# Gated feed-forward of a graph network on Trainium2: the order of VectorE's sums and splits in three of the four quads, and what GpSimd's last weight split waits for

## The chip, the cores and the metric

One core of a Trainium2 chip runs the whole program. The metric is the device time of one execution in microseconds (us). Its parts are named as in the profile: PE is TensorE's matmuls, PEld its weight loads, DVE is VectorE, ACT is ScalarE, POOL is GpSimd, SP is the engine that issues most DMAs.

## What is computed

The reference takes 1024 nodes with 512 features, normalises them, applies a graph convolution, then four layers of attention and a gated feed-forward network, and a second graph convolution. All is float32. The change lies in the feed-forward part of each layer. There, cut to what matters:

```
for i in range(L):                                   # L = 4, D = 512
    h = h + attention(_ln(h, ln2_w[i], ln2_b[i]), cond, Wq[i], Wk[i], Wv[i], Wo[i])
    u = _ln(h, ln3_w[i], ln3_b[i]) @ geglu_w[i] + geglu_b[i]   # 1024x512 @ 512x4096
    val, gate = jnp.split(u, 2, axis=-1)
    f = val * gelu(gate)                                       # 1024x2048
    h = h + f @ ffo_w[i] + ffo_b[i]
```

## The kernel before

The 2048 columns of `f` are four quarters, r = 0 to 3, of four column blocks of 128 (c = 0 to 3). Products with the gate and value weights are made by a seven-product scheme in the manner of Strassen (products 0 to 6 on sums and differences of blocks), so each block needs sums of products afterwards, and these sums are VectorE's.

**The first quarter** runs in float32, in four objects of class `Quad` (quads 0 to 3 below, c = 0 to 3). Products 0 and 1 are made early. `Quad.rest` makes the other five, each of four 128x512 matmuls (`multiply`, L301), into three PSUM banks b, c and d, and between them VectorE sums:

- product 5 into b, then u2 = b + s1 (the tile `gu`);
- product 6 into c, then u3 = c + u2 (also `gu`);
- product 4 into d, then g1 = d + u3 (`g`), which ScalarE passes through the gelu (L972);
- product 3 is added onto c, so TensorE may begin it only when u3 has read c; then g0 = c + u2;
- product 2 is added onto d, so TensorE may begin it only when g1 has read d; then d = d + u2, and the results fT (L1000, L1001), which go to DRAM.

I write c' and d' for products 3 and 2 (the second ones on banks c and d). All these sums are line L982 of VectorE. They read PSUM. In the trace the five products of a quad are `gb`, `gc`, `gd`, `gc`, `gd` of L301 in this order, so the second `gc` of a quad is c' and the second `gd` is d'.

**The fills.** `fill()` takes the next piece of a list of splits that the later quarters need: each float32 tile of the normalised input is split into a high and a low part. A piece is one VectorE instruction on 128x512 (L1017 writes `gr`, L1025 and L1037 write `gl`; both inputs lie in SBUF), at times with ScalarE work ahead of it (L1012, L1015). Behind each L1037 a GpSimd instruction (L1039) makes a third part. After quads 1, 2 and 3, `sums()` gives GpSimd four instructions on 128x256 (L1081) on the weights of a coming chunk. The order of all VectorE work here is that in which the code issues it. Before the change one fill stands behind u2, u3, g1 and g0 each, and one (in `rest`, the last) behind fT.

**The other quarters** are twelve objects of class `Chunk` (r = 1 to 3), with three matmuls on split operands for each product (L1109). The weights of a chunk are split by ScalarE, VectorE (L1045) and GpSimd (L1050: `gsa`, `gsb`, `gs`). `split_rest` issues the second half of a chunk's weight split, and its GpSimd part is made to wait for the VectorE instruction `split_left.low`. Chunk (3,3) is the last. In its stretch the output stage begins: `output.split(0, ...)` splits the first piece of `f` read back from DRAM by `left_parts`: ScalarE `ah_f` (L318), VectorE `al_f` (L319, 128x1024), GpSimd `as_f` (L321). The output's matmuls are L1252. VectorE's instruction L1127 (`scale_onto`) rewrites a PSUM bank that the chunk's next product is added onto; L1175 and L1177 make fT, L1144 the sums.

Of the kernel before, what the change touches and what calls it, by code (L numbers as in the profile page):

```python
# [15 lines left out]
OP = mybir.AluOpType  # L16
# [5 lines left out]
TINY = 2.0 ** -12  # L22
# [4 lines left out]
def gnn_kernel(  # L27
# [26 lines left out]
    nc = tc.nc  # L54
# [10 lines left out]
    KC = D // P  # L65
# [4 lines left out]
    R = DFF // D  # L70
# [156 lines left out]
    h = [hall[:, nb, :] for nb in range(NB)]  # L227
# [78 lines left out]
    def twelve_bits(t):  # L306
        return t.bitcast(F32R)
# [3 lines left out]

    def left_parts(x, name, t=None):

        parts = [slots_of(len(x), f"{n}_{name}") for n in ("ah", "al", "as")]
        for h, l, s, x in zip(*parts, x):
            nc.scalar.mul(twelve_bits(h), x, INWARD * TINY)  # L318
            nc.vector.scalar_tensor_tensor(twelve_bits(l), h, -1.0 / TINY, x, OP.mult, OP.add)  # L319
            if t:  # L320
                t.tensor_tensor(twelve_bits(s), h, l, OP.subtract)  # L321
                continue
            for k in range(2):
                nc.gpsimd.tensor_tensor(twelve_bits(s)[:, k, :], h[:, k, :], l[:, k, :],  # L324
                                        OP.subtract)
        return parts
# [619 lines left out]
    class Quad:  # L946
# [27 lines left out]
        def rest(self, fill):  # L974
            n, bias = self.n, gcols[:, self.cv:self.cv + 1]
            b, c, d = (bank(f"{x}_{n}") for x in ("gb", "gc", "gd"))
            u2, u3 = (acc_tile(f"g{x}_{n}") for x in ("u2", "u3"))
            g0, g1 = (t512(f"{x}_{n}") for x in ("g0", "g1"))
            f0, f1 = self.f.of(self.c)

            def add(to, x, y):
                self.last = pin(nc.vector.tensor_tensor(to, x, y, OP.add))  # L982

            self.product(5, b, True, pin)
            add(u2, b, self.s1)
            fill()
            self.product(6, c, True, pin)
            add(u3, c, u2)
            fill()
            self.product(4, d, True, pin)  # L990
            add(g1, d, u3)
            self.gate(g1, n)
            fill()
            self.product(3, c, False, pin)
            add(g0, c, u2)
            self.gate(g0, n)
            fill()
            self.product(2, d, False, pin)
            add(d, d, u2)
            pin(nc.vector.scalar_tensor_tensor(f0, self.a, bias, g0, OP.add, OP.mult))  # L1000
            pin(nc.vector.scalar_tensor_tensor(f1, d, bias, g1, OP.add, OP.mult))  # L1001
            self.f.store(self.c)
            fill()
            fill()
# [196 lines left out]
    class Output:  # L1201
# [8 lines left out]
                self.raw[n] = slot(f"fr_{self.l}_{n}")  # L1210
                nc.sync.dma_start(self.raw[n], f_dram[s, 2 * u:2 * u + 2].rearrange("c p n -> p c n"))

        def split(self, n, t=nc.vector):
            if n in self.raw:
                self.f[n] = left_parts([self.raw.pop(n)], f"f_{self.l}_{n}", t)

        def fetch_w(self, u):
            if u < UNITS:
# [206 lines left out]
    for l in range(L):  # L1425
# [231 lines left out]
        f, quads = quads_of(l, 0, left, right)  # L1657
# [28 lines left out]
        def fill(n=1):  # L1686
            for _ in range(n):
                next(parts, None)
# [64 lines left out]
                load()  # L1753
        sum_chunk(2)

        def split_rest(short):
            long = begin_split(0, False)
            next(long, None)
            with waiting_for(split_left.low, mybir.EngineType.Pool):
                for flow in short, long:  # L1760
                    for _ in flow:
                        pass

        output = Output(l)
        ahead = output.ahead()
        before, short = None, iter(())
        for r in range(1, R):
            f = Gated(l, r)
            for c in range(KC):
                n = (r - R + 2) * KC + c  # L1770
                if n == -1:
                    output.fetch_w(0)
                if (r, c) == (R - 1, KC - 2):
                    output.fetch(0)
                chunk = ready.pop(0)
                flow = chunk.steps(lambda: before and sum_chunk(1))
                chunk.f = f
                next(flow)
                if 0 < n < 5:
                    next(ahead)  # L1780
                for _ in islice(short, 2):
                    pass
                next(flow)
                if before:
                    split_rest(short)
                    load()
                for _ in parts:
                    pass
                if (r, c) == (R - 1, KC - 1):
                    with in_order(mybir.EngineType.Activation), in_order(mybir.EngineType.DVE), \  # L1790
                            in_order(mybir.EngineType.Pool):
                        output.split(0, nc.gpsimd)
                    output.fetch(1)
                for step in range(3):
                    if before:
                        next(before, None)
                    next(flow)
                    if step == 1 and not before:
                        split_rest(iter(()))
                        load()  # L1800
                before = flow
                short = begin_split(0, True)
                if n == 0:
                    next(ahead)
# [153 lines left out]
```

## Time and profile before

| | |
|---|---|
| median of 3 runs | 2298.52 us (2296.37 to 2298.68) |
| the profiled execution's own time | 2296.64 us |
| its span in the trace | 2294.9 us |
| granted TensorE clock | 1.000 |
| the four quads of layer 0 | 408 to 447 us in the span |
| the twelve chunks of layer 0 | 446 to 563 us |
| distance of a layer from the next | 529 us |

The profile's page gives busy times over the whole span. The timeline lists instructions in order of time: start, duration, engine, line, operation, tile written and tiles read, shape, count where several are merged; in brackets what the engine waited for before. A VectorE instruction's duration reaches some 0.08 us into the next one's, so spacing of starts is used where instructions follow each other. The four layers repeat: the first stall of the second quad stands at 425.48 in layer 0 and at 1483.01 two layers later.

### The profile page before, as it was taken

The numbers are of one execution on the slowest core, as the hardware profiler recorded it, in microseconds if no ns is written. First come the engines' busy times: TensorE is split into PE (matmuls) and PEld (weight loads), VectorE is DVE, ScalarE is ACT, GpSimd is POOL, SyncE is SP. The second block draws the span as 40 slices with busy tenths as digits, with TensorE's granted clock in tenths as the row PEclk, the third lists the DMA queues.
The fourth block names the chain that finished last, engine by engine and source line by source line (L and its number), as shares of the span: only waits on it lengthen the run. The fifth ranks groups of instructions, "written<-read, shape, count | busy, mean of one in ns | idle before, by whom it ended". The sixth has DMA issues, their size and how long they took to land. (4 is left out here: it accounts for less than half of the span.)

```text
span 2294.9 us, 34482 instructions
## 1 busy us (share of the span) xinstructions
PE 2265.4 (99%) x12496; PEld 1754.5 (76%) x12496; DVE 1734.6 (76%) x3172; ACT 1168.7 (51%) x2245; POOL 747.1 (33%) x647
## 2 busy tenths in 40 slices
PE   8999999999999999999999999999999999999999
PEld 5678887587887888488887888578788888668777
DVE  9886556999986555989987554989987554899965
ACT  7555445565355445465356444556437444556521
POOL 1121213486021224377021222368112112268301
PEclk9999999999999999999999999999999999999999
DMA  6042211234411101133521111133531111043551
GB/s 206 2 152 70 74 61 42 83 120 152 169 46 65 61 29 42 60 119 99 200 92 65 51 38 42 42 107 100 184 138 56 37 52 51 1 129 111 184 173 57
DMA packets 144113, 204.42 MB, mean 89 GB/s; under 512 B 11240, under 2 KB 68912, under 8 KB 143936
## 3 DMA queue, kind: packets, MB, share of 16 engines
q1 hardware_dynamic: 141840, 196.72, 26.0%
q0 software_dynamic: 1376, 4.30, 0.6%
q8 instruction: 103, 1.69, 0.3%
q10 hardware_dynamic: 720, 1.11, 0.1%
q14 instruction: 74, 0.61, 0.1%
HBM read 151.75 MB, written 50.34 MB: 88 GB/s over the span
## 5 line engine op out<-in xcount | busy, mean ns | idle before, releaser
L324 POOL TENSOR_TENSOR as_c<-ah_c,al_c 128x512 fp32r<-128x512 f32 x128 | 197.7, 1574 | 901.0 <-DVE al_c L319 679.9
L1123 ACT ACTIVATE g<-g 128x512 f32<-128x512 f32 x192 | 112.5, 586 | 152.8 <-PE g L1109 151.5
L381 ACT ACTIVATE k<-k 128x512 f32<-128x512 f32 x125 | 73.0, 585 | 193.0 <-PE k L370 193.0
L1252 PE MATMUL fx<-bs_wff,as_f 128*128 128x512 f32 x512 | 159.0, 390 | 0.6 <-DVE as_f L321 0.6
L1252 PE MATMUL fy<-bl_wff,al_f 128*128 128x512 f32 x512 | 158.8, 390 | 0.6 <-DVE al_f L319 0.5
L318 ACT ACTIVATE ah_f<-fr 128x1024 fp32r<-128x1024 f32 x64 | 67.9, 1061 | 177.3 <-PE fy L1252 98.8
L1252 PE MATMUL fy<-bh_wff,ah_f 128*128 128x512 f32 x512 | 157.8, 390 | 0.2 <-ACT ah_f L318 0.2
L386 DVE COPY kT<-k 128x512 f32<-128x512 f32 x54 | 37.2, 689 | 156.8 <-PE k L370 156.8
L370 PE MATMUL v<-bh_wv,ah_c 128*128 128x512 f32 x508 | 140.9, 399 | 0.0
L370 PE MATMUL v<-bs_wv,as_c 128*128 128x512 f32 x508 | 137.1, 393 | 2.6 <-ACT v L381 2.6
L1050 POOL TENSOR_TENSOR gsa<-gha,gla 128x512 fp32r<-128x512 f32 x96 | 124.1, 1315 | 40.2 <-DVE gla L1045 40.2
L370 PE MATMUL v<-bl_wv,al_c 128*128 128x512 f32 x508 | 136.6, 390 | 0.0
L843 ACT ACTIVATE pr<-sc,nmax 128x256 f32<-128x256 f32 x256 | 118.1, 474 | 35.0 <-DVE nmax L838 34.5
L370 PE MATMUL k<-ah_c,bh_wk 128*128 128x512 f32 x500 | 135.1, 392 | 0.0
L381 ACT ACTIVATE v<-v 128x512 f32<-128x512 f32 x127 | 75.0, 591 | 116.9 <-PE v L370 116.9
L370 PE MATMUL k<-as_c,bs_wk 128*128 128x512 f32 x500 | 132.1, 395 | 1.8 <-ACT k L381 1.8
L370 PE MATMUL k<-al_c,bl_wk 128*128 128x512 f32 x500 | 133.8, 389 | 0.0
L1109 PE MATMUL g<-gr,gha 128*128 128x512 f32 x384 | 120.0, 394 | 0.0
L1109 PE MATMUL g<-gr,gsa 128*128 128x512 f32 x384 | 119.9, 393 | 0.0
L1109 PE MATMUL g<-gl,gla 128*128 128x512 f32 x384 | 118.3, 389 | 0.0
L370 PEld LDWEIGHTS v<-bs_wv,as_c 128*128 128x128 f32 x508 | 93.2, 188 | 27.7 <-ACT v L381 5.7
L370 PEld LDWEIGHTS v<-bh_wv,ah_c 128*128 128x128 f32 x508 | 92.6, 188 | 27.9 <-issue 9.2
(321 smaller groups left out, 5814.3 us busy)
## 6 DMA issues: line engine op xcount, KB each, us to landing
f_dram<-fT SPq DMA_DIRECT2D x128, 256.0 KB, 2.1
fr<-f_dram SPq DMA_DIRECT2D x64, 512.0 KB, 4.1
ct<-cond_dram SPq DMA_DIRECT2D x48, 512.0 KB, 4.7
wff<-in_L_gnn_ffo_w_dram SPq DMA_DIRECT2D x32, 512.0 KB, 5.2
gxb<-in_L_gnn_geglu_w_dram SPq DMA_DIRECT2D x96, 128.0 KB, 2.5
gxa<-in_L_gnn_geglu_w_dram SPq DMA_DIRECT2D x96, 128.0 KB, 2.6
cond<-in_L_gnn_cond_dram SPq DMA_DIRECT2D x32, 256.0 KB, 4.2
cond_dram<-ct SPq DMA_DIRECT2D x16, 512.0 KB, 3.3
```

The costliest lines, as they stand in the source:

```text
L318: nc.scalar.mul(twelve_bits(h), x, INWARD * TINY)
L324: nc.gpsimd.tensor_tensor(twelve_bits(s)[:, k, :], h[:, k, :], l[:, k, :], OP.subtract)
L370: pin(nc.tensor.matmul(self.bank, twelve_bits(left[k // 2])[:, k % 2, self.c * P:(self.c + 1) * P], twelve_bits(right[k // 2])[:, k % 2, : ...
L381: nc.scalar.mul(self.bank, self.bank, 1.0 + TINY)
L386: nc.vector.tensor_copy(self.to(), self.bank)
L843: nc.scalar.activation(pr3[:, a, :], ps3[:, a, :], AF.Exp, bias=nmax[:, a:a + 1], accum_out=tot[:, a:a + 1])
L1050: split_left.last = pin(t.tensor_tensor(s_at, h_at, l_at, OP.subtract))
L1109: pin(nc.tensor.matmul(to, self.part(i, which)[:, k, :], self.rights[i][which].bitcast(F32R)[:, k, :], start=start and k == 0, stop=stop a ...
L1123: pin(nc.scalar.mul(to, to, 1.0 + TINY))
L1252: pin(nc.tensor.matmul(to, twelve_bits(left[which][0])[:, k, b * P:(b + 1) * P], twelve_bits(right[which])[:, k, :], start=u == 0 and whic ...
```

## The change

Two things are moved; no computation is added or taken away.

First, `Quad.rest`: in quads 1 and 2 (c = 1, 2) no fill stands between u2 and u3, and two stand behind u3. In quad 0 two fills stand between u2 and u3 where there was one. So all later fills come one place earlier in the list, until in quad 3 the list ends.

Second, at the last chunk `split_rest` is no longer called ahead of `output.split(0, ...)` but from inside it, between `al_f` and `as_f`, and GpSimd's part of it waits for `al_f`.

```
-    def left_parts(x, name, t=None):
+    def left_parts(x, name, t=None, between=None):
...
             nc.scalar.mul(twelve_bits(h), x, INWARD * TINY)
-            nc.vector.scalar_tensor_tensor(twelve_bits(l), h, -1.0 / TINY, x, OP.mult, OP.add)
+            left_parts.low = nc.vector.scalar_tensor_tensor(twelve_bits(l), h, -1.0 / TINY, x,
+                                                            OP.mult, OP.add)
+            if between:
+                between()
...
             self.product(5, b, True, pin)
             add(u2, b, self.s1)
-            fill()
+            at_once = self.c in (1, 2)
+            if not at_once:
+                fill()
+            if not self.c:
+                fill()
             self.product(6, c, True, pin)
             add(u3, c, u2)
+            if at_once:
+                fill()
             fill()
             self.product(4, d, True, pin)
             add(g1, d, u3)
...
-        def split(self, n, t=nc.vector):
+        def split(self, n, t=nc.vector, between=None):
             if n in self.raw:
-                self.f[n] = left_parts([self.raw.pop(n)], f"f_{self.l}_{n}", t)
+                self.f[n] = left_parts([self.raw.pop(n)], f"f_{self.l}_{n}", t, between)
...
-        def split_rest(short):
+        def split_rest(short, behind=None):
             long = begin_split(0, False)
             next(long, None)
-            with waiting_for(split_left.low, mybir.EngineType.Pool):
+            with waiting_for(behind or split_left.low, mybir.EngineType.Pool):
...
+                the_last = (r, c) == (R - 1, KC - 1)
                 if before:
-                    split_rest(short)
+                    if not the_last:
+                        split_rest(short)
                     load()
                 for _ in parts:
                     pass
-                if (r, c) == (R - 1, KC - 1):
+                if the_last:
                     with in_order(mybir.EngineType.Activation), in_order(mybir.EngineType.DVE), \
                             in_order(mybir.EngineType.Pool):
-                        output.split(0, nc.gpsimd)
+                        output.split(0, nc.gpsimd, lambda: split_rest(short, left_parts.low))
                     output.fetch(1)
```

On VectorE, this is quad 1 of layer 0 before the change, from its first fill pair to g1; `gu_0_0_1` is u2 (from bank `gb`) and u3 (from bank `gc`), `g_0_0_1` from `gd` is g1:

```order
L1001 SCALAR_TENSOR_TENSOR fT_0_0_18314<-gd_0_0_18309,gcols,g_0_0_0_18313 128x512
L1037 SCALAR_TENSOR_TENSOR gl_4_18331<-ln3S_0_17701,gr_4_18329 128x512
L1037 SCALAR_TENSOR_TENSOR gl_6_18354<-ln3T_1_0_17699,gr_6_18352 128x512
L982 TENSOR_TENSOR gu_0_0_1_18372<-gb_0_1_18369,gs_0_0_0_18128 128x512
L1037 SCALAR_TENSOR_TENSOR gl_6_18354<-ln3T_1_0_17699,gr_6_18352 128x512
L982 TENSOR_TENSOR gu_0_0_1_18373<-gc_0_1_18370,gu_0_0_1_18372 128x512
L1017 SCALAR_TENSOR_TENSOR gr_5_18383<-ln3S_1_17702,gt_5_0_18385 128x512
L982 TENSOR_TENSOR g_0_0_1_18375<-gd_0_1_18371,gu_0_0_1_18373 128x512
```

The same stretch of VectorE in the changed kernel (lines are numbered 3 or 9 higher there: L985 is L982, L1010 is L1001, L1026 is L1017, L1046 is L1037):

```order
L1010 SCALAR_TENSOR_TENSOR fT_0_0_18314<-gd_0_0_18309,gcols,g_0_0_0_18313 128x512
L1046 SCALAR_TENSOR_TENSOR gl_6_18347<-ln3T_1_0_17699,gr_6_18345 128x512 x2
L985 TENSOR_TENSOR gu_0_0_1_18379<-gb_0_1_18376,gs_0_0_0_18128 128x512
L985 TENSOR_TENSOR gu_0_0_1_18380<-gc_0_1_18377,gu_0_0_1_18379 128x512
L1026 SCALAR_TENSOR_TENSOR gr_5_18365<-ln3S_1_17702,gt_5_0_18367 128x512
L1026 SCALAR_TENSOR_TENSOR gr_5_18365<-ln3S_1_17702,gt_5_1_18391 128x512
L985 TENSOR_TENSOR g_0_0_1_18382<-gd_0_1_18378,gu_0_0_1_18380 128x512
```

u3 has moved ahead of one fill, and the place between u3 and g1 now holds two.

On VectorE in quad 2 of layer 0, before, from fT of quad 1 to g1:

```order
L1025 SCALAR_TENSOR_TENSOR gl_5_18398<-ln3S_1_17702,gr_5_18382 128x512
L1017 SCALAR_TENSOR_TENSOR gr_18412<-ln3S_2_17703,gt_3_0_18414 128x512
L982 TENSOR_TENSOR gu_0_0_2_18433<-gb_0_2_18430,gs_0_0_2_18166 128x512
L1017 SCALAR_TENSOR_TENSOR gr_18412<-ln3S_2_17703,gt_3_1_18417 128x512
L982 TENSOR_TENSOR gu_0_0_2_18434<-gc_0_2_18431,gu_0_0_2_18433 128x512
L1025 SCALAR_TENSOR_TENSOR gl_3_18442<-ln3S_2_17703,gr_18412 128x512
L982 TENSOR_TENSOR g_0_0_2_18436<-gd_0_2_18432,gu_0_0_2_18434 128x512
```

and in the changed kernel (L1034 is L1025):

```order
L1026 SCALAR_TENSOR_TENSOR gr_18405<-ln3S_2_17703,gt_3_0_18407 128x512
L1026 SCALAR_TENSOR_TENSOR gr_18405<-ln3S_2_17703,gt_3_1_18417 128x512
L985 TENSOR_TENSOR gu_0_0_2_18435<-gb_0_2_18432,gs_0_0_2_18166 128x512
L985 TENSOR_TENSOR gu_0_0_2_18436<-gc_0_2_18433,gu_0_0_2_18435 128x512
L1034 SCALAR_TENSOR_TENSOR gl_3_18420<-ln3S_2_17703,gr_18405 128x512 x2
L985 TENSOR_TENSOR g_0_0_2_18438<-gd_0_2_18434,gu_0_0_2_18436 128x512
```

Again u3 follows u2 at once, and two fills stand ahead of g1.

The orders of TensorE and of GpSimd stay as they were. Of the waits on GpSimd, these are the ones at the last chunk of layer 0, before (in brackets the engines whose semaphores are waited for):

```order
L1050 TENSOR_TENSOR gsa_3_3_19545<-gha_3_3_19543,gla_3_3_19544 128x512 [waits DMAHW1_49,DMAHW0_49,Activation_49]
L1050 TENSOR_TENSOR gsa_3_3_19545<-gha_3_3_19543,gla_3_3_19544 128x512
L1050 TENSOR_TENSOR gsb_3_3_19616<-ghb_3_3_19614,glb_3_3_19615 128x512 [waits DVE_49,PE_49]
L1050 TENSOR_TENSOR gs_0_3_3_19613<-gs_0_3_3_19613 128x256 [waits PE_49,Activation_49]
L321 TENSOR_TENSOR as_f_0_0_19637<-ah_f_0_0_19635,al_f_0_0_19636 128x1024 [waits DVE_49]
```

and in the changed kernel (L1059 is L1050, L324 is L321):

```order
L1059 TENSOR_TENSOR gsa_3_3_19545<-gha_3_3_19543,gla_3_3_19544 128x512 [waits DMAHW1_49,DMAHW0_49,Activation_49]
L1059 TENSOR_TENSOR gsa_3_3_19545<-gha_3_3_19543,gla_3_3_19544 128x512
L1059 TENSOR_TENSOR gsb_3_3_19616<-ghb_3_3_19614,glb_3_3_19615 128x512 [waits DVE_49,PE_49]
L1059 TENSOR_TENSOR gs_0_3_3_19613<-gs_0_3_3_19613 128x256 [waits PE_49,Activation_49]
L324 TENSOR_TENSOR as_f_0_0_19635<-ah_f_0_0_19633,al_f_0_0_19634 128x1024 [waits Activation_49]
```

`gsb` still waits for VectorE, but now for `al_f` where it was for the chunk's own low part; `as_f` no longer needs that wait, since it stands behind `gsb`.

Beside this, ScalarE issues one `gt` of the fills ahead of the gate of quad 2, and SP issues the four weight loads of the first chunk in the order gxa, gxa, gxb, gxb (before: gxb, gxa, gxa, gxb).

## Prediction

> **What bounds the kernel now.** I read the page's first part, then what TensorE waits for, then the timeline of TensorE in layer 0.
>
> ```profile
> PE 2265.4 (99%) x12496; PEld 1754.5 (76%) x12496; DVE 1734.6 (76%) x3172; ACT 1168.7 (51%) x2245; POOL 747.1 (33%) x647
> ```
>
> TensorE is busy 2265.4 of 2294.9 us, and the change takes no matmul away. Only TensorE's waits can shrink. The table of waits (us in total, times, longest) has two rows that the change can touch:
>
> ```profile
> PE gc L301 <- DVE gu L982: 4.4, 8, 0.7
> ...
> PE g L1109 <- DVE g L1127: 1.2, 4, 0.3
> ```
>
> Eight waits of c' for u3 are two a layer; four waits of a chunk's matmul for L1127 are one a layer. The timeline of TensorE in quads 1 to 3 shows where the first ones stand:
>
> ```profile
> 416.30 1.88 PE L301 MATMUL gc<-ln3S,wgate 128*128 128x512 f32 x4
> ...
> 423.16 1.88 PE L301 MATMUL gd<-ln3S,ges 128*128 128x512 f32 x4
> 425.48 1.98 PE L301 MATMUL gc<-ln3S,wgate 128*128 128x512 f32 x4 [0.43 <-DVE gu L982]
> 427.30 1.88 PE L301 MATMUL gd<-ln3T,ges 128*128 128x512 f32 x4
> 429.01 1.88 PE L301 MATMUL gb<-ln3S,ges 128*128 128x512 f32 x4
> ...
> 432.45 1.88 PE L301 MATMUL gd<-ln3S,ges 128*128 128x512 f32 x4
> 435.00 1.98 PE L301 MATMUL gc<-ln3S,wgate 128*128 128x512 f32 x4 [0.67 <-DVE gu L982]
> 436.82 1.88 PE L301 MATMUL gd<-ln3T,ges 128*128 128x512 f32 x4
> 438.53 1.88 PE L301 MATMUL gb<-ln3S,ges 128*128 128x512 f32 x4
> ...
> 441.97 1.88 PE L301 MATMUL gd<-ln3S,ges 128*128 128x512 f32 x4
> 443.80 1.56 PE L301 MATMUL gc<-ln3S,wgate 128*128 128x512 f32 x3
> ```
>
> The first row is quad 0's c', before any stall. An undisturbed product begins 1.72 us after the last (438.53 to 441.97 are two steps). c' of quad 1 begins 2.32 later, 0.60 lost, and its successor 1.82 later, 0.10 lost. In quad 2 the same sum is 0.83 + 0.10, in quad 3 0.11 + 0.10. Together 1.84 us a layer, 7.4 us in four: that is all that the first part can bring.
>
> **Part one: u3 earlier, g1 behind two fills.** These are VectorE's and GpSimd's rows in quad 1:
>
> ```profile
> 422.45 0.69 DVE L1037 SCALAR_TENSOR_TENSOR gl<-ln3T,gr 128x512 fp32r<-128x512 f32 x1
> 423.05 0.69 DVE L982 TENSOR_TENSOR gu<-gb,gs 128x512 f32<-128x512 f32 x1
> 423.65 1.17 DVE L1037 SCALAR_TENSOR_TENSOR gl<-ln3T,gr 128x512 fp32r<-128x512 f32 x1
> 424.74 0.68 DVE L982 TENSOR_TENSOR gu<-gc,gu 128x512 f32<-128x512 f32 x1
> 425.34 1.15 DVE L1017 SCALAR_TENSOR_TENSOR gr<-ln3S,gt 128x512 fp32r<-128x512 f32 x1
> 426.42 0.68 DVE L982 TENSOR_TENSOR g<-gd,gu 128x512 f32<-128x512 f32 x1
> ...
> 419.67 1.27 POOL L1039 TENSOR_TENSOR gr<-gl,gt 128x512 fp32r<-128x512 f32 x1 [7.78 <-ACT g L972]
> 422.68 4.95 POOL L1039 TENSOR_TENSOR gr<-gl,gt 128x512 fp32r<-128x512 f32 x3 [1.74 <-DVE gl L1037]
> ...
> 424.24 1.71 POOL L1039 TENSOR_TENSOR gr<-gl,gt 128x512 fp32r<-128x512 f32 x1
> ```
>
> A fill alone takes 0.69, its successor starting 0.60 behind it; beside a running GpSimd operation it takes 1.15 to 1.17. GpSimd's takes 1.27 alone and 1.71 beside fills. The sums, which read PSUM, keep 0.68 or 0.69 even at 423.05 and 424.74, where GpSimd is at work. So a fill and a GpSimd operation exclude each other, and a sum excludes nothing. The rows give the size: GpSimd's operation of 424.24 ends at 425.95, the fill that waited for it since 425.34 lets the next sum start at 426.42, 0.47 behind that end. And GpSimd, when it waits, really starts some 0.06 before the fill's successor (424.74 to 425.95 is 1.21 of its 1.27).
>
> In the changed kernel quad 0, which has no such wait, has one fill more between u2 and u3. Its cover: GpSimd is idle for 7.78 us there, so the fill costs VectorE 0.60, and u3 is done at about 415.5, before c' may begin anyway at 416.30 by TensorE's spacing. That costs nothing.
>
> Quad 1: both `gl_6` fills stand at 421.85 and 422.45, u2 at 423.05, u3 at 423.65 to 424.34. TensorE could begin c' at 424.88 (423.16 + 1.72), so the wait of 425.48 is gone, 0.60 earlier. Next d' needs g1, and ahead of g1 stand two fills from 424.25 on. GpSimd's two operations behind `gl_6` then run at 422.68 to 424.25 and from 424.25. Whoever goes first, 1.27 of GpSimd and two fills share the time: GpSimd to 425.52, the first fill ending for its successor at 425.99, the second at 426.59; or fill, GpSimd to 426.06, and the second fill at 426.53. So g1 starts at 426.53 to 426.59, against 426.42 before. It ends 0.68 later, and TensorE follows 0.06 behind (u3 424.74 + 0.68, c' 425.48): d' at 427.27 to 427.33, where it was at 427.30. **The wait has moved from c' to d'**, some 0.7 us at a place where none stood, and with the slow restart of 0.10 behind it quad 1 ends 0.07 to 0.14 later than before.
>
> Quad 2 has these rows on VectorE and GpSimd:
>
> ```profile
> 431.21 0.80 DVE L1025 SCALAR_TENSOR_TENSOR gl<-ln3S,gr 128x512 fp32r<-128x512 f32 x1
> 431.93 1.21 DVE L1017 SCALAR_TENSOR_TENSOR gr<-ln3S,gt 128x512 fp32r<-128x512 f32 x1
> 433.06 0.68 DVE L982 TENSOR_TENSOR gu<-gb,gs 128x512 f32<-128x512 f32 x1
> ...
> 434.26 0.68 DVE L982 TENSOR_TENSOR gu<-gc,gu 128x512 f32<-128x512 f32 x1
> ...
> 430.73 0.73 POOL L1081 TENSOR_TENSOR gy<-gxb,gxa 128x256 f32<-128x256 f32 x1
> 431.42 1.18 POOL L1081 TENSOR_TENSOR gxa<-gxa,gxb 128x256 f32<-128x256 f32 x1
> ```
>
> Here GpSimd makes the weight sums, 0.73 each when alone. It has one operation fewer in front of them, so they run some 1.2 us earlier. VectorE begins the two fills ahead of u2 at about 431.25, and by my count GpSimd's second sum of the second chunk falls due in the same tenth of a microsecond: its first four sums, in turn with the fills of quad 1, run from 426.5 to 430.2, the next takes 0.73, and the one behind it is due some 0.3 later, at 431.24. If the fill goes first, u2 starts at 432.99, u3 at 433.60, c' at 434.34 (before 435.00); the two fills ahead of g1 meet one GpSimd operation, g1 ends at 436.22, d' begins at 436.28 and the next product at 438.10, 0.43 earlier than before. If GpSimd goes first, u2 is at 433.57, c' at 434.91, the fills ahead of g1 run free, and the next product begins at 438.45, 0.08 earlier. In quad 3 u3 follows u2 too and the 0.21 there goes. So part one brings 0.29 to 0.64 a layer. No row decides the tie; I take 0.5, **2.0 us in four layers**. Without collisions it would be 1.84.
>
> The Trainium skill, page "SBUF — State Buffer", section "Who interferes with whom", states the same exclusion and speaks against this change: a VectorE instruction with two SBUF inputs and a GpSimd one that reads SBUF share a read interface, the first to issue keeps it throughout, and the other blocks. The rows above agree (1.15 against 0.69). The page's section "A bandwidth-pool intuition that's wrong (but worth ruling out)" gives about 115 ns from release to the blocked one's start, measured on descriptor writing; as an estimate from that page, a blocked fill's successor would start 0.72 behind GpSimd's end instead of the 0.47 of the rows, g1 of quad 1 would be 0.25 later, and a layer would lose that much more. The rows decide.
>
> **The moved loads.** SP issues the same four loads of chunk (1,0) at the same place, in another order. GpSimd's first sum needs a gxa and a gxb. I cost it at nothing, since GpSimd reads them behind its last L1039 operation; if it is free first, it starts when they land.
>
> ```profile
> 423.91 1.78 SPq L1071 DMA_DIRECT2D gxb<-in_L_gnn_geglu_w_dram  x3
> ...
> gxa<-in_L_gnn_geglu_w_dram SPq DMA_DIRECT2D x96, 128.0 KB, 2.6
> ```
>
> The first row is of SP's timeline, the second of the page's list of transfers, whose last number is the median time from issue to landing, 2.6 us. The last of the four loads is issued at 423.91, so it has landed by 426.5; the third, which in the new order completes the first pair, some 0.5 sooner, by 426.0. This is just when the second fill ahead of g1 takes its turn, the ground for a rival below.
>
> **Part two: GpSimd behind al_f.** The rows at the end of the chunks of layer 0:
>
> ```profile
> 554.91 1.30 POOL L1050 TENSOR_TENSOR gsb<-ghb,glb 128x512 fp32r<-128x512 f32 x1 [2.36 <-DVE gs L1045]
> 555.36 1.93 DVE L319 SCALAR_TENSOR_TENSOR al_f<-ah_f,fr 128x1024 fp32r<-128x1024 f32 x1 [0.59 <-ACT ah_f L318]
> 556.21 0.68 ACT L1136 ACTIVATE g<-g,gcols 128x512 f32<-128x512 f32 x1
> 557.22 0.74 DVE L1175 SCALAR_TENSOR_TENSOR fT<-g,gcols,g 128x512 f32<-128x512 f32 x1
> ...
> 561.33 0.61 PE L1109 MATMUL g<-gr,gsb 128*128 128x512 f32 x2
> 562.26 0.72 PE L1109 MATMUL g<-gr,gsb 128*128 128x512 f32 x2 [0.32 <-DVE g L1127]
> 562.95 0.70 PE L1109 MATMUL g<-gr,gs 128*128 128x512 f32 x2
> ...
> 564.42 0.62 PE L1252 MATMUL fx<-bs_wff,as_f 128*128 128x512 f32 x2
> 565.30 1.23 DVE L319 SCALAR_TENSOR_TENSOR al_f<-ah_f,fr 128x1024 fp32r<-128x1024 f32 x1
> ```
>
> `al_f` takes 1.93 beside `gsb` and 1.23 alone, 0.70 more. From it VectorE runs without a gap to the L1127 for which TensorE waits. With GpSimd behind it, `al_f` releases fT 0.70 earlier, at 556.5. But fT needs the gate that ScalarE ends at 556.89: it starts at 556.94, 0.28 earlier, and TensorE too, at 561.98. That is **1.1 us in four layers**; the whole loss at this place (562.26 is 0.48 behind the spacing of 0.45, and 0.3 follows) would be 0.8 a layer, 3.2 us.
>
> Its cost: GpSimd's `gsb` starts at 556.7 instead of 554.91, is done at 558.0, `gs` at 558.8, and `as_f`, queued behind, at 561.2 (2.40 us as before). TensorE reads them at 561.33, 562.95 and 564.42. The margins are 3.3, 4.2 and 3.2 us, so this costs nothing.
>
> **Sum.** Against the profiled execution: 2296.64 - 2.0 - 1.1 = 2293.5 us. The median is 1.9 us above the profiled execution, so I forecast 2295.4 against 2298.52. A change of this kernel under 0.2% (4.6 us) can hardly be told from none, so this is "within 0.2%".
>
> **Rivals.**
>
> *The fills ahead of g1 run free.* For it: 0.69 is what most fills take. Against it: GpSimd's second operation follows its first at 424.24 in the trace, at the moment that the fills begin. Then g1 starts at 425.46, d' follows c' unhindered, and all 7.4 us return: 2298.52 - 7.4 - 1.1 = 2290.0. Chance 0.22.
>
> *The fills ahead of g1 are blocked twice.* If the weight loads land before 426.0 in quad 1, or GpSimd holds its queue of sums against VectorE, a GpSimd operation of 0.73 gets in between the two fills, too. g1 of quad 1 then starts at 427.1, d' at 427.8, 0.6 later than before; in quad 2 both fills meet one, and d' begins at 437.3 against 436.82, 0.5 later. A layer loses 1.1 to 1.2, four 4.7, and with nothing from part two the time is 2303.2, slower. Against it: in the trace the two engines take turns, so that a waiting fill goes ahead of GpSimd's next operation (424.24, then 425.34, then the third). It decides only if a load lands 0.5 us sooner than the group's 2.6. Chance 0.10.
>
> *Part two does not do it.* If `al_f` is long because its input is late rather than because of `gsb`, nothing comes of it: 2296.5. Against it: the bracket of its row says that VectorE waited 0.59 for `ah_f` before it began, so the input was there when its 1.93 us started. Chance 0.13.
>
> The forecast itself has 0.50, and 0.05 are left to mixtures within the bound. Faster by over 0.2%: the first rival and a little of the mixtures, 0.23. Slower: 0.11. Within: 0.66. The range goes from the first rival's 2290.0 to 2300.5, which takes in a blocked fill in one of the two quads (about 2 us) and leaves out the full second rival.
>
> **What would show it.** In the trace of the changed kernel the row "gc <- gu" among TensorE's waits should nearly vanish, and a new row "gd <- g L985" stand there with some 0.7 us in each quad 1; g1 of quad 1 should start near 426.5, its second fill no earlier than 425.9. `al_f` of the last chunk should take 1.2, and TensorE's wait for L1127 shrink to about 0.04 a layer. If no row of `gd` appears, the exclusion was misjudged and the time is near 2290; if c' still waits, or d' over 1.2 us, it is near or above 2300.

## The result, and the profile after

The changed kernel takes 2293.27 us (median of 20 runs, 2292.49 to 2296.97), the one before 2296.77 (20 runs, 2296.16 to 2300.33). The ratio is 0.9983 with a 95% interval of 0.9976 to 0.9989: 0.17% faster, 3.5 us by the medians and 3.9 by the ratio. The profiled execution's span fell from 2294.9 to 2291.1 us.

TensorE's waits in the changed kernel (engine, tile, line, what it waited for: us in total, times, longest):

```profile
PE gd L301 <- DVE g L985: 2.2, 4, 0.5
...
PE gc L301 <- DVE gu L985: 0.2, 1, 0.2
```

The row of c' for u3, 4.4 us in eight waits before, has shrunk to one wait of 0.2. In its place stands a row that was not there: the second product on d waits for g1, once a layer, 0.5 us. The row of L1127 is gone. That a row is gone does not say that nothing is lost there: the spacing of starts in the timeline shows shorter waits that have no row and no bracket. The timeline of TensorE in quads 1 to 3 of layer 0:

```profile
423.07 1.88 PE L301 MATMUL gd<-ln3S,ges 128*128 128x512 f32 x4
424.79 1.88 PE L301 MATMUL gc<-ln3S,wgate 128*128 128x512 f32 x4
427.21 1.98 PE L301 MATMUL gd<-ln3T,ges 128*128 128x512 f32 x4 [0.55 <-DVE g L985]
429.03 1.88 PE L301 MATMUL gb<-ln3S,ges 128*128 128x512 f32 x4
...
432.46 1.88 PE L301 MATMUL gd<-ln3S,ges 128*128 128x512 f32 x4
434.42 1.98 PE L301 MATMUL gc<-ln3S,wgate 128*128 128x512 f32 x4
436.24 1.97 PE L301 MATMUL gd<-ln3T,ges 128*128 128x512 f32 x4
438.04 1.88 PE L301 MATMUL gb<-ln3S,ges 128*128 128x512 f32 x4
...
443.19 1.88 PE L301 MATMUL gc<-ln3S,wgate 128*128 128x512 f32 x4
```

All starts are 0.09 earlier than before already at 423.07 (it was 423.16), so 0.09 is to be added when the two timelines are compared. c' of quad 1 follows at once; d' begins 2.42 behind c' instead of 1.72, and the first product of quad 2 stands at 429.12 against 429.01: quad 1 is 0.11 slower than before. The whole gain comes behind it: c' of quad 2 begins 1.96 behind its predecessor (it was 2.55; undisturbed it is 1.72, so 0.24 is still lost), quad 3 has no wait, and its c' stands at 443.28 against 443.80. VectorE and GpSimd at the place where the wait went to:

```profile
422.96 0.68 DVE L985 TENSOR_TENSOR gu<-gb,gs 128x512 f32<-128x512 f32 x1
423.75 0.69 DVE L985 TENSOR_TENSOR gu<-gc,gu 128x512 f32<-128x512 f32 x1
424.36 1.60 DVE L1026 SCALAR_TENSOR_TENSOR gr<-ln3S,gt 128x512 fp32r<-128x512 f32 x1
...
424.36 2.20 DVE L1026 SCALAR_TENSOR_TENSOR gr<-ln3S,gt 128x512 fp32r<-128x512 f32 x2
426.48 0.68 DVE L985 TENSOR_TENSOR g<-gd,gu 128x512 f32<-128x512 f32 x1
...
422.61 2.79 POOL L1048 TENSOR_TENSOR gr<-gl,gt 128x512 fp32r<-128x512 f32 x2 [1.51 <-DVE gl L1046]
```

GpSimd has its two operations behind `gl_6` (part 6 below) without a gap until 425.40; the first fill ahead of g1 comes in at 424.36, must let the second of them end, and takes 1.60 us instead of 0.68. (The row with x2 is both fills ahead of g1 together.) g1 starts at 426.48. Ahead of u2 of quad 2, VectorE's two fills and GpSimd's weight sums:

```profile
431.15 1.81 DVE L1026 SCALAR_TENSOR_TENSOR gr<-ln3S,gt 128x512 fp32r<-128x512 f32 x2
...
426.71 0.72 POOL L1090 TENSOR_TENSOR gxa<-gxa,gxb 128x256 f32<-128x256 f32 x1 [1.31 <-PE gc L301]
...
430.54 0.74 POOL L1090 TENSOR_TENSOR gxa<-gxa,gxb 128x256 f32<-128x256 f32 x1
431.35 2.20 POOL L1090 TENSOR_TENSOR gxa<-gxa 128x256 f32<-128x256 f32 x2
```

The first fill begins at 431.15, 0.20 ahead of the sum of 431.35, and runs free; only the second meets GpSimd. GpSimd's first sum, at 426.71, stands behind 1.31 us of idle time. The bracket puts this down to TensorE, but the trace has the last of the four weight loads landing at 426.56, 0.15 ahead of the sum. The same 0.15 or 0.16 stands there in e1 (426.71, then 426.87), e3 (428.02, then 428.18) and e10 (428.96, then 429.12), and in e10 the product that the bracket would name (c' of quad 1, from 427.62 on for 1.98 us) was still running when the sum began. So it is this load that the sum waits for. At the end of the chunks:

```profile
554.61 1.23 DVE L319 SCALAR_TENSOR_TENSOR al_f<-ah_f,fr 128x1024 fp32r<-128x1024 f32 x1 [0.60 <-ACT ah_f L318]
555.98 1.30 POOL L1059 TENSOR_TENSOR gsb<-ghb,glb 128x512 fp32r<-128x512 f32 x1 [4.16 <-DVE al_f L319]
556.17 0.75 DVE L1184 SCALAR_TENSOR_TENSOR fT<-g,gcols,g 128x512 f32<-128x512 f32 x1 [0.34 <-ACT g L1145]
557.24 0.73 POOL L1059 TENSOR_TENSOR gs<-gs 128x256 fp32r<-128x256 f32 x1
557.94 2.40 POOL L324 TENSOR_TENSOR as_f<-ah_f,al_f 128x1024 fp32r<-128x1024 f32 x1
```

`al_f` takes 1.23, and now it is ScalarE's gate for which fT waits, 0.34 us. GpSimd's `gs` and `as_f` are done at 557.97 and 560.34; TensorE reads them at 561.91 and 563.37, 3.9 and 3.0 us later.

To compare runs I use two stretches of each layer that TensorE's timeline gives: **quads**, from the start of the layer's first matmul of L301 to the start of its last, and **chunks**, from there to the first matmul of the output stage. They are medians of the four layers of the one profiled execution of each kernel. The layers agree within 0.1 us, but for e10, whose quads take 57.53 to 57.81, and one layer of e7, whose chunks take 117.06. Before, layer 0 has 389.08, 446.92 and 563.50.

| kernel | median us | ratio to before, 95% interval | quads us | chunks us |
|---|---|---|---|---|
| before | 2296.77 | | 57.86 | 116.56 |
| the change | 2293.27 | 0.9983 (0.9976 to 0.9989) | 57.20 | 116.28 |
| e1_sums_only | 2295.62 | 0.9993 (0.9984 to 1.0002) | 57.20 | 116.53 |
| e2_split_only | 2295.65 | 0.9994 (0.9985 to 1.0003) | 57.84 | 116.28 |
| e3_one_ahead | 2295.24 | 0.9990 (0.9981 to 0.9999) | 57.49 | 116.31 |
| e4_third_later | 2292.16 | 0.9979 (0.9970 to 0.9988) | 56.93 | 116.30 |
| e5_second_sums_later | 2290.44 | 0.9969 (0.9957 to 0.9981) | 56.42 | 116.28 |
| e6_both_sums_later | 2292.63 | 0.9976 (0.9966 to 0.9986) | 56.68 | 116.30 |
| e7_order_before | 2299.01 | 1.0006 (0.9997 to 1.0015) | 58.23 | 116.53 |
| e8_no_extra_fill | 2298.21 | 1.0001 (0.9992 to 1.0010) | 58.19 | 116.28 |
| e9_sums_apart | 2291.12 | 0.9977 (0.9968 to 0.9986) | 55.96 | 117.12 |
| e10_extra_fill_only | 2296.64 | 0.9995 (0.9986 to 1.0004) | 57.64 | 116.30 |
| e11_sums_at_quad3 | 2288.80 | 0.9964 (0.9950 to 0.9977) | 55.95 | 116.28 |

Each experiment ran in turn with the kernel before, whose median was 2296.94 with e1 to e4, 2297.48 with e5 to e8, 2297.02 with e9 and e10, and 2297.81 with e11; the ratios are to these. There are 5 runs of e11, 6 of e5, 9 of e6 and 11 of each other one.

Four times the change of both stretches is 3.8 us for the change itself, which is the change of the span. The stretches say where time went to a tenth of a microsecond; the totals of the experiments, with intervals of 2 to 3 us to each side, only confirm it.

### The profile page after: what moved, and what is told of

It reads as the page before. It is cut to its first block, busy times and chain, and to the rows that moved or that the text cites. A ratio compares the mean times of both kernels' runs of the same rounds, so it can differ in the third digit from the quotient of the medians.

```text
span 2291.1 us, 34484 instructions
## 1 busy us (share of the span) xinstructions
PE 2264.6 (99%) x12496; PEld 1754.8 (77%) x12496; DVE 1730.9 (76%) x3172; ACT 1168.5 (51%) x2245; POOL 736.6 (32%) x647
## 5 line engine op out<-in xcount | busy, mean ns | idle before, releaser
L1059 POOL TENSOR_TENSOR gsa<-gha,gla 128x512 fp32r<-128x512 f32 x96 | 124.0, 1313 | 43.7 <-DVE gla L1054 43.7
```

The lines of the kernel that those rows point to most:

```text
L1059: split_left.last = pin(t.tensor_tensor(s_at, h_at, l_at, OP.subtract))
```

## Experiments

My theory is that of the prediction: a fill (VectorE, both inputs in SBUF) and a GpSimd operation exclude each other, and TensorE's waits in the quads come from fills that meet GpSimd's work ahead of u3 or g1. The rivals: the waits come from the place of u3 and g1 in VectorE's queue alone, or the gain is of one part only.

### The two parts alone

`e1_sums_only` undoes the second part:

```
-                    if not the_last:
-                        split_rest(short)
+                    split_rest(short)
...
-                        output.split(0, nc.gpsimd, lambda: split_rest(short, left_parts.low))
+                        output.split(0, nc.gpsimd)
```

> Part one alone: the fills of the first three quads as in the changed kernel, GpSimd's last weight split as before. Theory (the two parts are independent, each worth what its own place in the trace gained): in the two traces the product behind quad 2 begins 0.40 us earlier against the start of the quads and quad 3 loses 0.2 less, so 0.5 us a layer, 2.1 us in four: 2294.7 against 2296.8 before. TensorE's wait of gd for g stays at 2.2 us, that of gc for gu is gone, that of L1109 for L1127 is back at 1.2. Rival (part one only moves the wait and the whole gain is part two's): 2296.8, and the product behind quad 2 no earlier.

Measured: quads 57.20, chunks 116.53. The first part alone is worth all of the quads' 0.66 us a layer and none of the chunks' time. The total fell by 1.3 to 1.6 us, less than the 2.1 expected, with an interval that reaches from 3.7 less to 0.5 more; the quads' 0.66 in four layers is 2.6. TensorE's table is as expected, but that one wait of gc for gu, 0.2 us, is left as in the change:

```profile
PE gd L301 <- DVE g L985: 2.2, 4, 0.5
...
PE g L1118 <- DVE g L1136: 1.3, 4, 0.3
```

`e2_split_only` undoes the first part:

```
-            at_once = self.c in (1, 2)
-            if not at_once:
-                fill()
-            if not self.c:
-                fill()
+            fill()
...
-            if at_once:
-                fill()
             fill()
```

> Part two alone: GpSimd's last weight split behind al_f, the fills as before. Theory: al_f takes 1.23 instead of 1.93, TensorE's wait for L1127 goes, and the stretch from there to the output stage is 0.43 us shorter a layer as in the changed kernel's trace, 1.7 us in four: 2295.1 against 2296.8. TensorE's wait of gc for gu stays at 4.4. Rival by the working of the prediction (only the start of the waiting matmul moves, the rest of the loss stays): 0.28 a layer, 2295.7.

Measured: quads 57.84, chunks 116.28. The second part is worth 0.28 a layer, 1.1 us: the rival's figure, which was the prediction's, and not the 0.43 that I had read from single matmuls. `al_f` of the last chunk takes 1.23 us here, and 1.92 in e1, where `gsb` runs beside it. The two parts add up: 0.66 and 0.28 by themselves, and the same together.

### Is it the number of fills ahead of g1, or GpSimd?

`e3_one_ahead` changes only the numbers of fills of quad 1, from two ahead of g1 and one behind it to one and two. It writes the fills behind u2, u3 and g1 of each quad as a table; the change has (0, 2, 1) for quads 1 and 2.

```
+    FILLS = ((2, 1, 1), (0, 1, 2), (0, 2, 1), (1, 1, 1))
...
-            at_once = self.c in (1, 2)
-            if not at_once:
-                fill()
-            if not self.c:
+            ahead_of = FILLS[self.c]
+            for _ in range(ahead_of[0]):
                 fill()
             self.product(6, c, True, pin)
             add(u3, c, u2)
-            if at_once:
+            for _ in range(ahead_of[1]):
                 fill()
-            fill()
             self.product(4, d, True, pin)
             add(g1, d, u3)
             self.gate(g1, n)
-            fill()
+            for _ in range(ahead_of[2]):
+                fill()
```

> The changed kernel, but in quad 1 one fill ahead of g1 and two behind it, instead of two and one. Theory (d' of quad 1 waits for g1, and g1 for two fills and what is left of a GpSimd operation): without the second fill g1 starts 0.60 earlier, at 425.9 in layer 0, d' at 426.6, its wait falls from 0.55 to 0.1 or nothing. That is 0.6 us a layer, 2.4 in four, less what GpSimd's sums take back in quad 2, whose fills then meet them in another order (up to 0.4 a layer): 2290.9 to 2292.5, against 2293.3 for the changed kernel. Rival (the wait of d' does not hang on that fill, or quad 2 gives all back): 2293.3.

Measured: quads 57.49, slower than the change by 0.3 a layer, against both. Quad 1 did what the theory said: d' loses 0.10 instead of 0.70. But quad 2 gave back more than that:

```profile
426.32 1.88 PE L301 MATMUL gc<-ln3S,wgate 128*128 128x512 f32 x4
428.14 1.98 PE L301 MATMUL gd<-ln3T,ges 128*128 128x512 f32 x4
...
436.24 1.13 PE L301 MATMUL gc<-ln3S,wgate 128*128 128x512 f32 x2 [0.97 <-DVE gu L987]
...
432.86 1.93 DVE L1026 SCALAR_TENSOR_TENSOR gr<-ln3S,gt 128x512 fp32r<-128x512 f32 x2
434.72 0.68 DVE L987 TENSOR_TENSOR gu<-gb,gs 128x512 f32<-128x512 f32 x1
...
432.38 0.73 POOL L1090 TENSOR_TENSOR gxa<-gxa,gxb 128x256 f32<-128x256 f32 x1
433.19 2.19 POOL L1090 TENSOR_TENSOR gxa<-gxa 128x256 f32<-128x256 f32 x2
```

TensorE is 0.6 us sooner at quad 2, but VectorE is not. Counted from the first product on d of quad 1 (424.60 here, 423.07 in the change), the fills ahead of u2 begin 0.18 later, since a fill of quad 1 met GpSimd for longer (1.21 us, where the change has 0.91), and they take 1.93 together instead of 1.81. So u2 and u3 are 0.3 later while TensorE needs u3 0.6 sooner: c' waits 0.97 and loses 1.13 against the change's 0.24. Whether a place pays depends on where GpSimd stands at that moment.

`e4_third_later` keeps the change's order and moves only GpSimd's two operations on part 6 behind g1 of quad 1:

```
-            pin(nc.gpsimd.tensor_tensor(s.bitcast(F32R)[:, k, :], low[:, k, :], less[k],
-                                        OP.subtract))
+            def third(k=k):
+                pin(nc.gpsimd.tensor_tensor(s.bitcast(F32R)[:, k, :], low[:, k, :], less[k],
+                                            OP.subtract))
+            if name.endswith("_6"):
+                held.append(third)
+            else:
+                third()
...
             add(g1, d, u3)
+            if held:
+                with waiting_for(self.last, mybir.EngineType.Pool):
+                    while held:
+                        held.pop(0)()
```

> The changed kernel, but GpSimd's two operations on part 6 wait for g1 of quad 1, so that they no longer run beside the two fills ahead of it. Theory (fill and GpSimd operation exclude each other): the two fills take 0.69 each instead of 1.60 and 0.68, g1 starts at about 425.6 and d' at 426.5 without a wait: 0.7 us a layer gained in quad 1. GpSimd is busy with the two operations 2.5 us longer afterwards, its weight sums come later and meet the fills of quad 2 as in the kernel before: 0.3 to 0.7 lost there. Sum 2290.5 to 2293.3. Rival (the first fill is long for a reason of its own, its input or its place): it stays at 1.6 and d' waits as before, and the time is 2293.3 or more.

Measured: 2292.16, quads 56.93, 0.27 a layer below the change. VectorE's rows decide between the theory and its rival:

```profile
424.45 1.28 DVE L1030 SCALAR_TENSOR_TENSOR gr<-ln3S,gt 128x512 fp32r<-128x512 f32 x2
425.65 0.68 DVE L985 TENSOR_TENSOR g<-gd,gu 128x512 f32<-128x512 f32 x1
...
426.48 3.27 POOL L1055 TENSOR_TENSOR gr<-gl,gt 128x512 fp32r<-128x512 f32 x2 [5.28 <-DVE g L985]
```

The same two fills at the same place take 1.28 together instead of 2.20, g1 starts at 425.65, and d' follows c' by 1.72. The order of the fills did not change, only GpSimd's work beside them. Much of this gain is lost in quad 2, where the sums now meet the second fill ahead of g1, which takes 1.21 us (a wait of d' of 0.3, 1.4 us in all).

### Moving GpSimd's sums

`e5_second_sums_later` adds this to e4: the sums for the second chunk wait for g1 of quad 2 (inside `rest`, like the held operations).

```
+        def sums_later():
+            sum_chunk(1)
...
-            q.rest(fill_first if c == KC - 1 else fill)
+            q.rest(fill_first if c == KC - 1 else fill, sums_later if c == 2 else None)
...
             if c == 2:
-                sum_chunk(1)
                 load()
```

> The changed kernel with GpSimd's two operations on part 6 behind g1 of quad 1, and its four sums for the second chunk behind g1 of quad 2. Theory (each fill that meets a GpSimd operation is some 0.6 us longer, and nothing else delays g1): without those sums the two fills ahead of g1 of quad 2 take 0.69 each instead of 0.68 and 1.21, d' of quad 2 loses its wait of 0.35 and the slow restart. That is 0.4 to 0.6 us a layer less than with part 6 alone, 1.6 to 2.4 in four: 2289.8 to 2290.6. Rival (the sums are needed early, and the first chunks wait for them instead): a new wait of the chunks' matmuls or of their splits as long as what is gained, 2292.2 or more.

Measured: 2290.44, quads 56.42, 0.51 a layer below e4, and chunks unchanged at 116.28: as the theory had it. TensorE's table has no row of L301 any more, but c' of quad 2 still comes 1.98 behind its predecessor, since the second fill ahead of u2 meets the first chunk's sums (1.21 us).

`e6_both_sums_later` has `sum_chunk(0)` there as well.

> As the run beside it, with GpSimd's sums for the first chunk behind g1 of quad 2 as well. Theory: the fill ahead of u2 of quad 2 also runs free, u3 starts 0.25 us or more sooner than TensorE needs it, and no product of the four quads waits but for the restart: 0.25 to 0.35 a layer less than the run beside it, 2288.6 to 2289.6, and the four quads take what they would without any wait. Rival: the first chunk's sums come 6 us later, its split with them, and TensorE waits at the start of the chunks: the time is above the run beside it.

Measured: 2292.63, quads 56.68, 0.26 above e5, against the theory and by another way than the rival's: quads 1 and 2 are free of waits, the chunks do not suffer, but the eight sums reach into quad 3 and its u3 is late:

```profile
442.74 1.98 PE L301 MATMUL gc<-ln3S,wgate 128*128 128x512 f32 x4 [0.43 <-DVE gu L985]
```

`e9_sums_apart` therefore leaves only `sum_chunk(0)` behind g1 of quad 2 and moves the second chunk's sums behind the loop over the quads, which is behind the first chunk's weight split in GpSimd's queue:

```
             if c == 2:
-                sum_chunk(1)
                 load()
+        sum_chunk(1)
         sum_chunk(2)
```

> The changed kernel with GpSimd's operations on part 6 behind g1 of quad 1, its sums for the first chunk behind g1 of quad 2, and its sums for the second chunk behind the whole of the quads and the first chunk's split. Theory: with both sums behind quad 2, quads 1 and 2 ran without a wait and only u3 of quad 3 was late (0.43 and the restart), because its fills met the second chunk's sums; with these out of the way no product of the quads waits: 0.5 us a layer less than there, 2288.3 to 2290 against 2296.9 before. Rival (the second chunk's sums now stand in GpSimd's queue between two weight splits, and its own split comes late): TensorE waits in the second or third chunk, L1109's lines, and the stretch of the chunks grows from 116.3 by 0.5 or more; 2290.4 or above.

Measured: 2291.12. Theory and rival were both right: quads 55.96, with no wait of L301 left in TensorE's table, and chunks 117.12, 0.84 longer than in e11. In layer 0 half a microsecond of it is lost in the first chunk: ScalarE's split of the second chunk's weights waits 0.74 us for GpSimd's late sums (L1104), ScalarE's next scaling of a bank (L1146) is 0.38 later than in e11, and TensorE waits for that. The rest comes at 519 and 529 us, in later chunks; its cause is open. The row of the first wait, which of the other runs only e7 has, once:

```profile
PE g L1132 <- ACT g L1146: 0.9, 4, 0.3
```

`e11_sums_at_quad3` moves the same sums in front of that split again, behind u2 of quad 3. Against e9:

```
             add(u2, b, self.s1)
+            if behind_u2:
+                with waiting_for(self.last, mybir.EngineType.Pool):
+                    behind_u2()
...
-            q.rest(fill_first if c == KC - 1 else fill, sums_later if c == 2 else None)
+            q.rest(fill_first if c == KC - 1 else fill, sums_later if c == 2 else None,
+                   (lambda: sum_chunk(1)) if c == KC - 1 else None)
...
-        sum_chunk(1)
         sum_chunk(2)
```

> As the run with all sums apart, but GpSimd's sums for the second chunk stand ahead of the first chunk's weight split again, behind u2 of quad 3. Theory: the four quads stay free of waits (56.0 us from the first to the last product of the quads, against 57.9 before and 57.2 in the changed kernel), since the fills of quad 3 are over by then; the sums then delay the first chunk's weight split by up to 1.5 us, which is ahead of TensorE's need by more than that or not: the chunks take 116.3 to 116.8. Sum 2288.3 to 2290.4. Rival (any place for these sums costs what it frees, as GpSimd's queue is needed at once for the first chunk): the chunks take 117 or g1 of quad 3 comes late, and the time is 2291 or more.

Measured: 2288.80, 0.9964 of the kernel before, the lowest median of all, though the intervals of other runs overlap its own; by the stretches it is 0.47 a layer below e5 and 0.85 below e9. Quads 55.95, chunks 116.28, no wait of L301 in the table. Every product of quads 1 to 3 follows the last by 1.72:

```profile
425.42 1.88 PE L301 MATMUL gc<-ln3S,wgate 128*128 128x512 f32 x4
427.14 1.88 PE L301 MATMUL gd<-ln3T,ges 128*128 128x512 f32 x4
428.85 1.88 PE L301 MATMUL gb<-ln3S,ges 128*128 128x512 f32 x4
...
434.00 1.88 PE L301 MATMUL gc<-ln3S,wgate 128*128 128x512 f32 x4
435.72 1.88 PE L301 MATMUL gd<-ln3T,ges 128*128 128x512 f32 x4
...
442.59 1.88 PE L301 MATMUL gc<-ln3S,wgate 128*128 128x512 f32 x4
```

### The order of fills, taken apart

`e7_order_before` is the kernel before, with its own order, and GpSimd moved: the held operations as in e4, for parts 4 and 6, and both sums behind g1 of quad 2 as in e6.

```
+            if name.endswith(("_4", "_6")):
+                held.append(third)
```

> The kernel before, its order of fills and its last weight split untouched, with GpSimd taken out of the way: its operations on parts 4 and 6 that are issued behind quad 0's g1 wait for g1 of quad 1, its sums for the first two chunks wait for g1 of quad 2. Theory (the waits of c' in the kernel before come mostly from fills that are long beside GpSimd, not from the place of u3): c' of quad 1 waits 0.1 instead of 0.43 (0.2 lost instead of 0.70 with the restart), c' of quad 2 0.1 to 0.4 instead of 0.67, as GpSimd's four held operations still meet some of its fills: 0.6 to 1.0 us a layer, 2292.9 to 2294.5 against 2296.9. Rival (the place of u3 behind a fill makes the wait, whatever GpSimd does): TensorE's waits of gc for gu stay near 4.4 and the time at 2296.9.

Measured: 2299.01, quads 58.23, 0.37 a layer slower, and TensorE's waits of gc for gu at 6.0. That is the opposite of what the theory foretold for the total. Its timeline:

```profile
425.68 1.98 PE L301 MATMUL gc<-ln3S,wgate 128*128 128x512 f32 x4
427.50 1.88 PE L301 MATMUL gd<-ln3T,ges 128*128 128x512 f32 x4
...
435.55 1.98 PE L301 MATMUL gc<-ln3S,wgate 128*128 128x512 f32 x4 [1.02 <-DVE gu L982]
...
444.88 1.98 PE L301 MATMUL gc<-ln3S,wgate 128*128 128x512 f32 x4 [0.48 <-DVE gu L982]
```

Quad 1 is as foretold: with GpSimd silent, c' begins 1.83 behind its predecessor (423.85 in that run), 0.11 lost and not 0.60, in the old order. In quads 2 and 3 the moved work meets the fills in front of u2 instead (one takes 1.75 us in quad 2, one 1.22 in quad 3), and u3 comes late. So in quad 1 the rival is refuted; over the whole, this moving of GpSimd does not pay with the old order. With e11's places for GpSimd the old order was not run, so it is not shown that only the new order can profit.

`e8_no_extra_fill` leaves out the extra fill of quad 0. It is e3 with another table:

```
+    FILLS = ((1, 1, 1), (0, 2, 1), (0, 2, 1), (1, 1, 1))
```

> The changed kernel without the extra fill of quad 0: all fills one place later in the list. Theory: in quad 1 the fills ahead of g1 are then the second of part 6 and the first of part 5, and GpSimd still owes two operations there, so g1 is as late as in the changed kernel (d' waits 0.5 again); GpSimd's sums come later by one operation and meet quad 2 as in the kernel before, where c' loses 0.3 to 0.6 more. 2293.3 to 2295.5. Rival (the extra fill is what makes room in quad 1): d' waits over 1.1 and the time is 2296 or more.

Measured: 2298.21, quads 58.19: slower than the change by 1.0 a layer and than the kernel before by 0.33. d' of quad 1 waits 0.54, as foretold; in quad 2 c' waits 0.30 and d' 0.35 on top. There the fill ahead of u2 and one ahead of g1 take 1.21 us each beside GpSimd's sums. The total is above my range, as I had counted on c' alone in quad 2; it lies where the rival had it, but the rival's sign, d' of quad 1 waiting over 1.1, did not come.

`e10_extra_fill_only` keeps the extra fill, with one fill behind u2 and one behind u3 in quads 1 and 2. It, too, is e3 with another table:

```
+    FILLS = ((2, 1, 1), (1, 1, 1), (1, 1, 1), (1, 1, 1))
```

> The changed kernel with the extra fill of quad 0, but with a fill between u2 and u3 in quads 1 and 2 and one behind u3, as before. Theory: in quad 1 the fill between u2 and u3 meets GpSimd's first operation on part 6 as a fill did in the kernel before, so c' loses 0.6 to 0.7 again; quad 2 gains 0.1 or 0.2 from GpSimd's earlier sums and quad 3 loses nothing, as u3 follows u2 there: 0.3 us a layer for the quads and 0.3 for GpSimd's last split, 2294.2 to 2295 against 2296.9 before and 2293.3 for the whole change. Rival (the extra fill alone is what helps, since it clears VectorE's queue): 2293.3 or less, and no wait of gc for gu.

Measured: 2296.64, quads 57.64: 0.22 below before and 0.44 above the change; the total is above my range, but its interval holds it. In quad 1 the fill between u2 and u3 meets GpSimd and takes 1.17, and c' waits 0.43, exactly as in the kernel before:

```profile
425.80 1.17 DVE L1026 SCALAR_TENSOR_TENSOR gr<-ln3S,gt 128x512 fp32r<-128x512 f32 x1
426.88 0.68 DVE L987 TENSOR_TENSOR gu<-gc,gu 128x512 f32<-128x512 f32 x1
```

In quad 2 of layer 0 c' waits 0.76, where it was 0.67; what is gained comes in quad 3, where the list of fills is at its end and u3 follows u2.

So neither half of the first part carries it: the extra fill alone brings 0.22 us a layer, u3 behind u2 alone loses 0.33, both together bring 0.66.

## Why the prediction was right

It said 2295.4 from 2298.52, 3.1 us less; measured are 3.5 us less by the medians, 3.8 by the stretches. Of the 2.1 us by which the time itself, 2293.27, lies below the forecast, 1.75 are the start: 2298.52 was the median of 3 runs, and 20 runs gave 2296.77.

- **Quad 1, the wait moves from c' to d'.** Right, in place and size: d' was foretold at 427.27 to 427.33, it is at 427.30 (427.21 and the 0.09 by which this execution is ahead), and the quad ends 0.11 later, within 0.07 to 0.14. GpSimd's operation went first. e4 shows the cause: without it the same fills take 1.28 and not 2.20. The handover of 0.47 held: g1 at 426.48 is one free fill (0.60) and 0.48 behind GpSimd's end at 425.40. By the 115 ns of the Trainium skill, page "SBUF — State Buffer", section "A bandwidth-pool intuition that's wrong (but worth ruling out)", the estimate was 0.72; the trace does not bear that figure out for this pair of engines, while it does bear out the exclusion of the section "Who interferes with whom".
- **Quad 2, a tie.** The fill went first (the change's fills ahead of u2 take 1.81 us together, one free and one beside GpSimd), so the upper end of 0.29 to 0.64 a layer held; measured are 0.66, just above it. The 0.5 that I had taken was a middle between the two, not a reading. It was less of a tie than I had counted: my count began GpSimd's sums at 426.5, and they began at 426.71, 426.80 with the 0.09, so that the sum in question came 0.2 behind the fill (431.35 against 431.15) and not 0.01 ahead of it. One detail was off: the two fills ahead of g1 met no GpSimd operation there, and c' began 0.17 later than foretold because u3, directly behind u2, starts 0.79 behind it and not 0.60. The two cancel.
- **Quad 3.** The 0.21 went, as foretold.
- **The second part.** 0.28 a layer, as foretold and for the reason given: `al_f` is as short as foretold, and fT now waits for ScalarE's gate.
- **The loads in another order.** No wait of TensorE came of it; it was not tried by itself. That the third load completes what GpSimd's first sum needs, from 426.0 on, was misread: the sum waited for the last of the four, which landed at 426.56. By then the second fill ahead of g1 had been under way since 425.88, so no second operation of GpSimd could get in ahead of it.
- **The first rival** (fills run free, 2290.0) is what e11 gives once GpSimd is out of the way: 1.91 a layer in the quads, against the ceiling of 1.84 that I had added up. **The slower rival** did not come, but e3 and e8 show its kind of loss: fills that meet GpSimd at a place where TensorE waits for what stands behind them.

## What to carry to other kernels

Where two engines exclude each other, an order of instructions on one of them is good or bad only against the other's timetable: putting u3 directly behind u2 lost 0.33 us a layer without the extra fill, gained 0.66 with it, and 1.91 with the other engine's work moved too. When a wait vanishes from the table of waits, look for the next consumer behind the work that was pushed back; here the freed c' was paid for by d'. Moving the engine that nobody waits for, by giving its work something to wait for, brought 1.25 us a layer on top of the 0.66 of the reordering (e11); in another place, and with the old order, it lost 0.37 (e7). And do not take a table of waits without a row for a stretch without a loss: e5 and e11 both have no row of L301, and their quads differ by 0.47 us.

## What the runs showed of the hardware

Two VectorE sums of which the second reads the first's result, u2 and u3, start 0.78 to 0.79 us apart when nothing stands between them (422.96 and 423.75 in the changed kernel, and in every run that has such a pair), while fills, and a sum behind a fill, start 0.60 apart, as do two sums of a chunk of which neither reads the other's result (559.29 and 559.88 in the changed kernel). With a fill between the two, as before the change, this costs nothing.

A fill that arrives just behind the start of a GpSimd operation is held for nearly its whole length: 1.60 us (424.36, GpSimd's operation having begun at 424.14) in the changed kernel, against 1.15 to 1.17 in the kernel before, where the fill arrived when the operation was well under way.
